# A cross-attention kernel's fill: one set of context values beside each of the first three slots, and the output weights loaded two slots later

## The chip, the cores and the metric

The kernel runs on one core of one Trainium2 chip. The metric is the device time of the whole kernel in microseconds (us), lower is better; a time of a kernel is the median of several runs. Before the change it is 1691.91 us, the median of three runs from 1691.86 to 1692.5 us.

## The reference

For 32 batches, hidden states of 512 rows by 640 columns attend to a context of 77 rows by 1024 columns, with 20 heads of 32 columns. Everything is float32.

```python
end = N_TXT                                   # 77
ehs_txt = encoder_hidden_states[:, :end]      # all the rows that there are
q = _heads(hidden_states @ to_q_w)
h_txt = _sdpa(q, _heads(ehs_txt @ to_k_w), _heads(ehs_txt @ to_v_w))
...
out = _merge(h_txt) + SCALE_OBJ * _merge(h_obj) + SCALE_OTH * _merge(h_oth) + SCALE_IP * _merge(h_ip)
out = out @ to_out_w + to_out_b
out = (out + residual) / RESCALE
```

The context has 77 rows, so the slices for the other three attentions are empty and add zeros. What is left is: queries, keys and values from three projections, softmax over 77 keys for each of 20 heads, the weighted values, an output projection, a bias and the residual.

## The kernel before, in words

**Precision.** Every large product is made from operands split into a high part (rounded to the matmul format) and a low part (the remainder); a product is three matmuls, high by high, high by low and low by high. ScalarE (ACT) makes the high part, VectorE (DVE) or GpSimd (POOL) the low one.

**Context first.** The 2464 context rows are taken in five groups (four of 512, the last of 416). For each group the keys (tile pk) and the values (tile pv) of five chunks of 128 columns, that is four heads each, are made on TensorE (PE) and put into DRAM (`k_dram`, `v_dram`). One chunk's values of a group are `context_values(g, j, psv)`: 24 matmuls, then a transposition on DVE into tile vs (`split_values`) and four DMAs from POOL's queue to `v_dram`. The value weights lie in two tiles, wv_s0 for chunks 0 to 2 and wv_s1 for chunks 3 and 4. Values of the last group are not needed before the last batches, and are put between the first steps of the attention.

**Attention by units.** A unit n is four heads of one batch: n = 5 b + j for batch b and chunk j, 160 units. The steps of a unit:
- `queries(n)`: 15 matmuls into tile pq, copied to tile qt (`copy_q`).
- `scores(n)`: 16 small matmuls into four PSUM banks, one a head. The banks are usually the four of tag sc; table `LENT` names the units for which some heads lie in a bank of tag po or pa.
- `maxima(n)` on DVE (tile nm), then `exps(n, i)` for head i: four exponentials on ACT into tile pn; a bank is free once the exponentials of its head are done.
- `normalize(n)`: a reciprocal on DVE (rs) that needs all of the unit's exponentials, and a product on POOL.
- `transpose_p(n)`: DVE transposes pn into tile z. There are two of each, pn0, z0 for even n and pn1, z1 for odd n.
- `move_p(n)`: four DMAs from SP's queue carry z into tile raw (two buffers), and so over the partitions.
- `values(n)`: four matmuls of raw with the batch's values (vb) into a bank pa; `high_a` on ACT and `low_a` on DVE split it into tile at, after which the bank is free.
- the output projection of a batch (`group`), from at and the output weights wo_s, which come from `wo_dram` by five DMAs (`load_wo`).

**Order.** The order is written by hand: an engine carries out its instructions in the order in which the code names them. Units 0 to 7 are the fill: `slot(n)` makes the scores of unit n, the queries of n + 1 and, from n = 3 on (`LAG`), the values of n - 3. From unit 8 (`FIRST`) on, `window(n)` takes two units at a time, 76 times, and `end()` closes. In the slots 3 to 6 (`copied`) `transpose_p(n - 1)` and `move_p(n - 1)` stand behind the copy of the queries. Memory is handed on by pools: wo_s lies where wv_s0 was, z1 and raw lie where wv_s1 and the context tiles ct were, and each waits for the last reader of what it lies on. In the kernel before, the last group's values are placed so: chunks 0 and 1 ahead of slot 0, chunk 2 in slot 0, chunks 4 and 3 in slot 1, none in slot 2. `load_wo` is called in slot 1, and slot 3's scores use one bank po, one pa and two sc.

Of the kernel before, what the change touches and what calls it, by code (L numbers as in the profile page):

```python
# [37 lines left out]
def kernel(  # L38
# [30 lines left out]
    NC_ = C // P  # L69
# [136 lines left out]
    def values_of(g, j, pool):  # L206

        for k in range(NK):
            values_of_chunk(g, j, k, pool)

    def split_values(g, j, between=None):

        g0, gn = GROUPS_KV[g]
        na = gn // Q
        vs = kvp.tile([P, G // Q, HD], F32, tag="vs", name="vs", bufs=3)
        nc.vector.transpose(vs[:, :na], pvs.pop(j)[:, :gn].rearrange("p (a d) -> p a d", d=HD))
        if between is not None:
            between()
        dst = v_dram[g0 : g0 + gn, j].rearrange("(a t) i d -> i t a d", t=Q)
        engine = nc.gpsimd if g == LAST else nc.sync  # L220
        for i in range(HPC):
            engine.dma_start(dst[i], vs[i * Q : (i + 1) * Q, :na])

    def context_values(g, j, pool):
        values_of(g, j, pool)
        split_values(g, j)
# [10 lines left out]
    def load_x(b, quarters=range(4)):  # L237

        if b not in xss:
            xss[b] = natural()  # L240
        xs = xss[b]
        src = x[b].rearrange("(a j) (q u) -> q j a u", j=Q, q=4)
        for q in quarters:
            nc.sync.dma_start(xs[q * Q : (q + 1) * Q, :, :], src[q])
# [64 lines left out]
    LAST, split_ks = len(GROUPS_KV) - 1, []  # L309
# [79 lines left out]
    psv = tc.alloc_tile_pool(name="psv", bufs=3, space=PSUM, side="right", reuse_waits="tile")  # L389
# [28 lines left out]
    def load_keys(b):  # L418
        nc.sync.dma_start(kbs[b % 2], k_dram[:, :, b * NKEY : (b + 1) * NKEY])

    def load_values(b):
        rows = v_dram[b * NKEY : b * NKEY + KPAD]
        nc.sync.dma_start(
            vbs[b % 2].rearrange("p j h d -> p (j h d)"),
            rows.rearrange("(c i) j h d -> i c (j h d)", i=Q),
        )

    def bank(tag):
        pool, bufs = (ps, {"sc": 4, "pq": 1}[tag]) if tag in ("sc", "pq") else (late[1], {"po": 1, "pa": 2}[tag])
        return pool.tile([P, S], F32, tag=tag, name=tag, bufs=bufs)  # L430
# [17 lines left out]
    def copy_q(n, copy=nc.scalar.copy):  # L448
        copy(qt_of(n), pqs.pop(n))  # L449
# [13 lines left out]
    def scores(n):  # L463
        banks = [bank(LENT.get(n, {}).get(i, "sc")) for i in range(HPC)]
        views = [sc.rearrange("p (t k) -> p t k", t=NQ)[:, :, :NKEY] for sc in banks]
        for t in range(NQ):
            for i in range(HPC):
                scs[n, i, t] = views[i][:, t]
                score(views[i][:, t], n, i, t)
        return views  # L470

    def maxima(n, views):
        for i in range(HPC):
            nm = nmt[:, (n % 2 * HPC + i) * NQ : (n % 2 * HPC + i + 1) * NQ]
            nc.vector.tensor_reduce(nm, views[i], AX.X, ALU.max, negate=True)
            for t in range(NQ):
                nms[n, i, t] = nm[:, t : t + 1]
# [53 lines left out]
    def transpose_p(n):  # L531

        pn, z = pnb[n % 2], zs[n % 2]
        nc.vector.transpose(  # L534
            z.rearrange("p c h t j -> p (h t) c j"),
            pn.rearrange("p a (c i) -> p a c i", i=Q),
        )

    def move_p(n):

        raws[n] = late[0].tile([KPAD, NQ, HPC, P], F32, tag="raw", name="raw", bufs=2)
        for a in range(4):
            nc.sync.dma_start(
                raws[n][:, a].rearrange("p h q -> p (h q)"),
                zs[n % 2][a * Q : (a + 1) * Q].rearrange("i c h t j -> i c (h t j)"),
            )
# [23 lines left out]
    def low_a(n):  # L570
        at = ats[n]
        nc.vector.tensor_tensor(
            at[:, 1, :], pas.pop(n), at[:, 0, :].bitcast(F32), ALU.subtract
        )
# [75 lines left out]
        elif h == 1:  # L650
            nc.sync.dma_start(out[last, rows, :], xr)

    LATE, LAG = 2, 3
    EARLY_X = {4: 0, 6: 1}
    LENT = {3: {0: "po", 1: "pa"}, 4: {2: "po", 3: "pa"}, 6: {2: "po", 3: "pa"}}
    held, wos = [], []

    def take(m, tag="pa"):
# [4 lines left out]
    def load_wo(ks):  # L663
        for k in ks:
            nc.sync.dma_start(wos[0][:, k].bitcast(F32), wo_dram[:, k].bitcast(F32))

    def slot(n, beside=()):
        b, j = divmod(n, NC_)
        copied, last = 3 <= n <= 6, n == FIRST - 1
        views = scores(n)  # L670
        maxima(n, views)
        while held:
            low_a(held.pop())
        if n and not copied and not last:
            transpose_p(n - 1)
        if n == 1:
            load_wo(range(3))
        if j == 0:
            load_keys(b + 1)
        if j == 1:  # L680
            load_values(b)
        if n == 1:
            load_wo(range(3, NC_))
        if n == 0:
            load_x(2)
            load_y(0, range(4))
        for i in range(2):
            exps(n, i)
        if last:
            transpose_p(n - 1)  # L690
        if n >= LATE and not last and not copied:
            move_p(n - 1)
        if len(beside) > 1:
            context_values(LAST, beside[1], psv)
        queries(n + 1, "po" if last else "pq")
        copy_q(n + 1, nc.vector.tensor_copy)
        if copied:
            transpose_p(n - 1)
            move_p(n - 1)
        if n >= LAG and not last:  # L700
            values(n - LAG)
        if last:
            qts.append(late[0].tile([P, S], F32, name="qt1"))
            queries(n + 2)
            copy_q(n + 2, nc.vector.tensor_copy)
        for i in range(2, HPC):
            exps(n, i)
        if not last:
            normalize(n)
        if n == 1:  # L710
            for i in range(NQ):
                transpose_x(2, i)
        if beside:
            context_values(LAST, beside[0], psv)
        if n >= LAG and not last:
            high_a(n - LAG)
            held.append(n - LAG)
        if n in EARLY_X:
            split_x(2, EARLY_X[n])
        if n == 3:  # L720
            load_bias()
        if n < 3:
            split_x(1, n + 2)
# [156 lines left out]
    for c in range(2):  # L880
        split_x(1, c)
    context_values(LAST, 1, psv)
    slot(0, (2,))
    kva.release()
    lw = ctx.enter_context(tc.tile_pool(name="lw", bufs=1, reuse_waits="tile"))
    wos.append(lw.tile([P, NC_, 2, C], FPR, name="wo_s"))
    slot(1, (3, 4))
    psv.release()
    kvp.release()
    late.append(ctx.enter_context(tc.tile_pool(name="late", bufs=1, reuse_waits="tile")))  # L890
# [2 lines left out]
    )  # L893
    zs.append(late[0].tile(ZSHAPE, F32, name="z1"))
    move_p(0)
    for n in range(LATE, FIRST):
        slot(n)
    for n in range(FIRST, N, 2):
# [42 lines left out]
```

## Time and profile before

| | |
|---|---|
| median of three runs | 1691.91 us |
| the profiled execution's own time | 1692.86 us |
| span of its profile | 1690.8 us |
| context stage (keys and values of the first four groups, keys of the last) | 0 to 249.7 us |
| first queries and the values of chunks 0 and 1 | 249.7 to 262.3 us |
| fill, slots 0 to 7 | 262.3 to 323.4 us |
| a window (two units) in the steady part | 17.63 us (scores at 323.37 and at 341.00) |
| busy share of the span: PE, DVE, ACT, POOL | 100%, 60%, 64%, 59% |

The span runs from the first to the last instruction of one profiled execution; 2.06 us of that execution lie outside it. Rows of the timeline give the start and the duration of one instruction or of a run of equal ones, both in us; in square brackets stands how long the engine was idle before it and what ended the wait. Ends of matmuls are modelled, so intervals between starts are the safer reading.

### The profile page before, as it was taken

How to read it: one execution, taken by the hardware profiler on the slowest of the kernel's cores; microseconds unless marked ns; L12 is line 12 of the kernel's file. 1: busy time of each engine (PE TensorE's matmuls, PEld its weight loads, DVE VectorE, ACT ScalarE, POOL GpSimd, SP SyncE). 2: the span in 40 equal slices, each digit the busy share in tenths (PEclk: the TensorE clock that was granted, in tenths of full speed). 3: DMA queues.
4: the chain of work that ended last, by engine and by line, in shares of the span. 5: the costliest groups of instructions: out<-in, count | busy, mean ns of one | idle time of the engine just before them, and what ended most of it. 6: DMA issues, size and time to landing. Idle time of an engine off the chain costs nothing.

```text
span 1690.8 us, 36827 instructions
## 1 busy us (share of the span) xinstructions
PE 1683.6 (100%) x12460; PEld 1303.9 (77%) x12460; DVE 1010.5 (60%) x1635; ACT 1075.9 (64%) x5622; POOL 990.1 (59%) x663
## 2 busy tenths in 40 slices
PE   9999999999999999999999999999999999999999
PEld 7888898777777777777777777777777777777777
DVE  4341235766676666766666657576666766667653
ACT  3231125867677676776767767677676776767762
POOL 1000026667667666667575766767667676766755
PEclk9999999999999999999999999999999999999999
DMA  9847558678889787879797988888979788888956
GB/s 182 159 94 189 121 103 229 150 173 188 190 187 204 172 204 175 202 181 212 166 211 166 211 181 195 185 194 186 203 173 204 173 202 190 188 192 183 210 136 187
DMA packets 363852, 306.51 MB, mean 181 GB/s; under 512 B 88784, under 2 KB 292112, under 8 KB 363664
## 3 DMA queue, kind: packets, MB, share of 16 engines
q1 hardware_dynamic: 360864, 296.61, 78.4%
q0 software_dynamic: 2704, 7.38, 1.4%
q8 instruction: 99, 1.62, 0.4%
q14 instruction: 89, 0.73, 0.1%
q10 hardware_dynamic: 96, 0.16, 0.0%
HBM read 120.36 MB, written 57.88 MB: 105 GB/s over the span
## 4 chain that ended last, share of the span: by engine, by line
PE 97%; DMA 1%; ACT 0%; DVE 0%; SPq 0%; issue 0%; POOL 0%; DVEq 0%; ACTq 0%
PE pq L437 32%; PE po L602 31%; PE pv L182 7%; PE pk L182 7%; PE sc L454 6%; PE po L553 4%; PE pq L553 4%; PE pa L454 3%; DMA wraw<-in_L_xattn_to_k_w_dram 1%; PE sc L634 1%; PE pa L553 0%; ACT pn L515 0%; DMA cs<-in_ctx_dram 0%; PE pa L634 0%; PE pq L602 0%; SPq L99 0%
## 5 line engine op out<-in xcount | busy, mean ns | idle before, releaser
L515 ACT ACTIVATE pn<-sc,nm 128x77 f32<-128x77 f32 x1928 | 597.3, 367 | 131.4 <-DVE nm L508 102.8
L437 PE MATMUL pq<-xt,wq_s 128*128 128x512 f32 x2349 | 559.0, 390 | 0.0
L602 PE MATMUL po<-at,wo_s 128*128 128x512 f32 x2295 | 554.6, 393 | 0.0
L437 PEld LDWEIGHTS pq<-xt,wq_s 128*128 128x128 f32 x2349 | 440.6, 188 | 91.4
L602 PEld LDWEIGHTS po<-at,wo_s 128*128 128x128 f32 x2295 | 425.1, 188 | 90.8
L515 ACT ACTIVATION_READ_ACCUMULATOR pn<-sc,nm 128x1 f32 x1928 | 477.3, 249 | 0.0
L527 POOL TENSOR_TENSOR pn<-pn,rs 128x1232 f32<-128x1232 f32 x160 | 363.6, 2273 | 125.3 <-DVE rs L525 121.8
L616 POOL TENSOR_TENSOR xs<-xs,ot 128x512 f32<-128x512 f32 x155 | 199.8, 1289 | 322.1 <-DVE ot L612 314.4
L534 DVE STREAM_TRANSPOSE z<-pn 128x1536 f32<-128x1536 f32 x160 | 282.3, 1765 | 113.7 <-POOL pn L527 92.2
L259 POOL TENSOR_TENSOR xt<-xs,xt 128x512 fp32r<-128x512 f32 x157 | 198.5, 1293 | 35.8 <-ACT xt L258 35.8
L515 ACT ACTIVATE pn<-pa,nm 128x77 f32<-128x77 f32 x620 | 200.5, 382 | 0.0
L587 POOL TENSOR_TENSOR xs<-xs,bias_y 128x640 f32<-128x640 f32 x124 | 192.4, 1574 | 0.2
L567 ACT CAST at<-po 128x512 fp32r<-128x512 f32 x77 | 45.1, 585 | 230.1 <-PE po L553 230.1
L508 DVE TENSOR_REDUCE nm<-sc 128x6 f32<-128x462 f32 x304 | 177.1, 624 | 15.2 <-PE pa L454 15.2
L449 DVE COPY qt<-pq 128x512 f32<-128x512 f32 x83 | 57.4, 691 | 210.1 <-PE pq L437 210.1
L454 PE MATMUL sc<-kb,qt 32*128 32x77 f32 x3856 | 161.9, 273 | 0.0
L515 ACT ACTIVATION_READ_ACCUMULATOR pn<-pa,nm 128x1 f32 x620 | 161.0, 263 | 0.0
L454 PEld LDWEIGHTS sc<-kb,qt 32*128 32x128 f32 x3856 | 149.4, 187 | 4.2 <-issue 2.2
L182 PE MATMUL pk<-ct,wk_s 128*128 128x512 f32 (+1 forms) x600 | 134.0, 382 | 0.7 <-ACT wk_s L89 0.5
L182 PE MATMUL pv<-ct,wv_s 128*128 128x512 f32 (+1 forms) x600 | 134.2, 382 | 0.0
L454 PEld LDWEIGHTS pa<-kb,qt 32*128 32x128 f32 x1240 | 83.9, 186 | 63.7 <-ACT at L567 63.7
L182 PEld LDWEIGHTS pk<-ct,wk_s 128*128 128x128 f32 x600 | 112.1, 188 | 20.9 <-ACT wk_s L89 1.2
(81 smaller groups left out, 1339.7 us busy)
## 6 DMA issues: line engine op xcount, KB each, us to landing
raw<-z SPq DMA_DIRECT2D x640, 192.0 KB, 3.4
xs<-in_x_dram SPq DMA_DIRECT2D x256, 320.0 KB, 6.3
out_dram<-xs SPq DMA_DIRECT2D x127, 320.0 KB, 4.8
vb<-v_dram SPq DMA_DIRECT2D x32, 240.0 KB, 4.4
kb<-k_dram SPq DMA_DIRECT2D x32, 192.5 KB, 4.6
cs<-in_ctx_dram SPq DMA_DIRECT2D x12, 512.0 KB, 9.0
k_dram<-ks POOLq DMA_DIRECT2D x20, 256.0 KB, 2.5
v_dram<-vs SPq DMA_DIRECT2D x80, 64.0 KB, 2.4
```

The source lines that it names most:

```text
L182: nc.tensor.matmul(held[j][:, :gn], w[:, k, a, :], cts[g, k][:, c, :gn], start=(k == 0 and n == 0), stop=(k == NK - 1 and n == 2),)
L259: low.tensor_tensor(parts[1], src, parts[0].bitcast(F32), ALU.subtract)
L437: nc.tensor.matmul(pqs[n], wq_s[:, k, a, j * P : (j + 1) * P], xts[b, k][:, c, :], start=(k == 0 and m == 0), stop=(k == NC_ - 1 and m == 2),)
L454: nc.tensor.matmul(out, qt_of(n)[r, t * P : (t + 1) * P], kbs[b % 2][r, j, :], start=True, stop=True, tile_position=(i * HD, 0),)
L508: nc.vector.tensor_reduce(nm, view, AX.X, ALU.max, negate=True)
L515: nc.scalar.activation(pnb[n % 2][:, at, :NKEY], scs.pop((n, i, t)), AF.Exp, bias=nms.pop((n, i, t)), accum_out=sms[n][:, at : at + 1],)
L527: nc.gpsimd.tensor_tensor(pf, pf, rs.unsqueeze(2).to_broadcast([P, NQ * HPC, NKEY]), ALU.mult)
L534: nc.vector.transpose(z.rearrange("p c h t j -> p (h t) c j"), pn.rearrange("p a (c i) -> p a c i", i=Q),)
L553: nc.tensor.matmul(pas[n][i * HD : (i + 1) * HD, :].rearrange("p (a q) -> p a q", q=P), vb[:, i, :], raw[:, :, i, :], start=True, stop=Tru ...
L587: nc.gpsimd.tensor_tensor(part, part, biases[1].unsqueeze(1).to_broadcast([P, 4, U]), ALU.add)
L602: nc.tensor.matmul(pos[b, c], wos[0][:, k, a, c * P : (c + 1) * P], ats[b * NC_ + k][:, d, :], start=(k == 0 and m == 0), stop=(k == NC_ - ...
L616: nc.gpsimd.tensor_tensor(part, part, ots.pop((b, c)).rearrange("p (a i) -> p a i", i=Q), ALU.add)
```

## The change

The last group's values of chunks 3, 4 and 2 stand in slots 0, 1 and 2, one set in each, at the place behind `normalize`. The output weights are loaded in slot 3 (three of five parts) and in slot 4 (two), behind `move_p`, where before all five were loaded in slot 1. Slot 3's scores use the four banks of tag sc. Since wv_s1 and ct are now read until slot 2 ends, z1 and raw exist only from there on: `transpose_p(1)` and `move_p(1)` stand between slot 2 and slot 3, where before they were in slot 2.

```diff
-    LATE, LAG = 2, 3
+    LATE, LAG = 3, 3
+    WO = {3: range(3), 4: range(3, NC_)}
     EARLY_X = {4: 0, 6: 1}
-    LENT = {3: {0: "po", 1: "pa"}, 4: {2: "po", 3: "pa"}, 6: {2: "po", 3: "pa"}}
+    LENT = {4: {2: "po", 3: "pa"}, 6: {2: "po", 3: "pa"}}
...
         while held:
             low_a(held.pop())
-        if n and not copied and not last:
-            transpose_p(n - 1)
         if n == 1:
-            load_wo(range(3))
+            transpose_p(0)
         if j == 0:
             load_keys(b + 1)
         if j == 1:
             load_values(b)
-        if n == 1:
-            load_wo(range(3, NC_))
...
-        if n >= LATE and not last and not copied:
-            move_p(n - 1)
-        if len(beside) > 1:
-            context_values(LAST, beside[1], psv)
         queries(n + 1, "po" if last else "pq")
         copy_q(n + 1, nc.vector.tensor_copy)
         if copied:
             transpose_p(n - 1)
             move_p(n - 1)
+        if n in WO:
+            load_wo(WO[n])
         if n >= LAG and not last:
             values(n - LAG)
...
-        if beside:
-            context_values(LAST, beside[0], psv)
+        for c in beside:
+            context_values(LAST, c, psv)
...
     context_values(LAST, 1, psv)
-    slot(0, (2,))
+    for n, c in enumerate((3, 4, 2)):
+        slot(n, (c,))
     kva.release()
     lw = ctx.enter_context(tc.tile_pool(name="lw", bufs=1, reuse_waits="tile"))
     wos.append(lw.tile([P, NC_, 2, C], FPR, name="wo_s"))
-    slot(1, (3, 4))
     psv.release()
     kvp.release()
...
     zs.append(late[0].tile(ZSHAPE, F32, name="z1"))
     move_p(0)
+    transpose_p(1)
+    move_p(1)
     for n in range(LATE, FIRST):
         slot(n)
```

How the instructions move, at three places. The number behind a tile's name tells two buffers apart: wv_s_82 is wv_s0, wv_s_83 is wv_s1; z_1877 and pn_1871 are z0 and pn0, z_2224 (now z_2283) and pn_1873 are z1 and pn1; qt_1875 is the one query tile of the fill.

PE from the scores of slot 0 to the first scores of slot 3, before:

```order
L454 MATMUL sc<-kb_1867,qt_1875 128x77 x16
L437 MATMUL pq<-xt,wq_s 128x512 x15
L182 MATMUL pv<-ct,wv_s_82 128x416 x24
L454 MATMUL sc<-kb_1867,qt_1875 128x77 x16
L182 MATMUL pv<-ct,wv_s_83 128x416 x24
L437 MATMUL pq<-xt,wq_s 128x512 x15
L182 MATMUL pv<-ct,wv_s_83 128x416 x24
L454 MATMUL sc<-kb_1867,qt_1875 128x77 x16
L437 MATMUL pq<-xt,wq_s 128x512 x15
L454 MATMUL po<-kb_1867,qt_1875 128x77
L454 MATMUL pa<-kb_1867,qt_1875 128x77
L454 MATMUL sc<-kb_1867,qt_1875 128x77 x2
```

and after the change, to the first values:

```order
L454 MATMUL sc<-kb_1867,qt_1875 128x77 x16
L437 MATMUL pq<-xt,wq_s 128x512 x15
L182 MATMUL pv<-ct,wv_s_83 128x416 x24
L454 MATMUL sc<-kb_1867,qt_1875 128x77 x16
L437 MATMUL pq<-xt,wq_s 128x512 x15
L182 MATMUL pv<-ct,wv_s_83 128x416 x24
L454 MATMUL sc<-kb_1867,qt_1875 128x77 x16
L437 MATMUL pq<-xt,wq_s 128x512 x15
L182 MATMUL pv<-ct,wv_s_82 128x416 x24
L454 MATMUL sc<-kb_1867,qt_1875 128x77 x16
L437 MATMUL pq<-xt,wq_s 128x512 x15
L553 MATMUL pa<-raw,vb_1869 32x512 x4
```

A set of values (pv) now stands between the queries and the scores three times; before, the last queries and the scores of slot 3 had nothing between them.

DVE from the scores' maxima of slot 2 to those of slot 3, before:

```order
L216 STREAM_TRANSPOSE vs<-pv 128x416
L475 TENSOR_REDUCE nm<-sc 128x4 x4
L534 STREAM_TRANSPOSE z_2224<-pn_1873 128x16x3x32
L449 COPY qt_1875<-pq 128x512
L525 RECIPROCAL rs<-sm 128x16
L475 TENSOR_REDUCE nm<-po 128x4
L475 TENSOR_REDUCE nm<-pa 128x4
L475 TENSOR_REDUCE nm<-sc 128x4 x2
```

and after:

```order
L216 STREAM_TRANSPOSE vs<-pv 128x416
L475 TENSOR_REDUCE nm<-sc 128x4 x4
L449 COPY qt_1875<-pq 128x512
L525 RECIPROCAL rs<-sm 128x16
L216 STREAM_TRANSPOSE vs<-pv 128x416
L534 STREAM_TRANSPOSE z_2283<-pn_1873 128x16x3x32
L475 TENSOR_REDUCE nm<-sc 128x4 x4
```

The last transposition of values and the one of unit 1's probabilities now stand directly ahead of the maxima of slot 3.

SP's queue of DMAs from the values of batch 0 on, before:

```order
L665 DMA wo_s<-wo_dram 128x1280 x3
L423 DMA vb_1869<-v_dram 96x1x640
L665 DMA wo_s<-wo_dram 128x1280 x2
L543 DMA raw<-z_1877 96x1x512 x4
L543 DMA raw<-z_2224 96x1x512 x4
L543 DMA raw<-z_1877 96x1x512 x4
L543 DMA raw<-z_2224 96x1x512 x4
L419 DMA kb_1867<-k_dram 128x5x77
```

and after:

```order
L423 DMA vb_1869<-v_dram 96x1x640
L543 DMA raw<-z_1877 96x1x512 x4
L543 DMA raw<-z_2283 96x1x512 x4
L543 DMA raw<-z_1877 96x1x512 x4
L666 DMA wo_s<-wo_dram 128x1280 x3
L543 DMA raw<-z_2283 96x1x512 x4
L666 DMA wo_s<-wo_dram 128x1280 x2
L419 DMA kb_1867<-k_dram 128x5x77
```

Three parts of the output weights now stand ahead of the move of unit 3, and two behind it.

## The prediction

> **What bounds the kernel now.** I read the page first, then who waited for whom from 240 to 330 us (PE appears there once), then the timeline of the fill engine by engine. The page's first part, and one row of the windows view for the steady part (its first two numbers are the length and PE's busy time), say who sets the end:
>
> ```profile
> PE 1683.6 (100%) x12460; PEld 1303.9 (77%) x12460; DVE 1010.5 (60%) x1635; ACT 1075.9 (64%) x5622; POOL 990.1 (59%) x663
> 323.30:1645.00 1321.70, 1321.70 (x10504) 1004.02 (x10500) 859.83 (x1391) 952.84 (x5173) 900.58 (x570) 1.00 0.83 188
> ```
>
> PE never stops in the windows, at a granted clock of 1.00. A change to the fill can therefore only shift the start of the windows; what reaches the first scores of window 8, at 323.37 us, reaches the end. Here is PE in the fill (start, duration, and in brackets a wait and what ended it):
>
> ```profile
> 262.28 1.13 PE L454 MATMUL sc<-kb,qt 32*128 32x77 f32 x32
> 263.34 3.68 PE L437 MATMUL pq<-xt,wq_s 128*128 128x512 f32 x15
> 266.86 4.69 PE L182 MATMUL pv<-ct,wv_s 128*128 128x416 f32 x24
> 271.48 1.13 PE L454 MATMUL sc<-kb,qt 32*128 32x77 f32 x32
> 272.54 4.75 PE L182 MATMUL pv<-ct,wv_s 128*128 128x416 f32 x24
> 277.13 3.58 PE L437 MATMUL pq<-xt,wq_s 128*128 128x512 f32 x15
> 280.55 4.69 PE L182 MATMUL pv<-ct,wv_s 128*128 128x416 f32 x24
> 285.17 1.13 PE L454 MATMUL sc<-kb,qt 32*128 32x77 f32 x32
> 286.23 3.68 PE L437 MATMUL pq<-xt,wq_s 128*128 128x512 f32 x15
> 290.69 0.33 PE L454 MATMUL po<-kb,qt 32*128 32x77 f32 x1 [0.78 <-DVE qt L449]
> 291.75 3.72 PE L437 MATMUL pq<-xt,wq_s 128*128 128x512 f32 x15
> ```
>
> From 262.28 us on the only idle time is 0.78 us before the scores of slot 3, whose query tile has to be copied by DVE. So the most that this stage can give is under a microsecond, 0.05% of the span. The differences that decide are differences of tenths, and the question is whether another engine lets PE keep them.
>
> **The change part by part.** *PE: the wait goes.* The same matmuls run, only their order differs, so I sum intervals between starts. Scores take 1.06 us (271.48 to 272.54), queries behind scores 3.52 (263.34 to 266.86), a set of values behind queries 4.62 (280.55 to 285.17). From slot 1's scores at 271.48 the new order is scores, queries, values, scores, queries, values: 2 x (1.06 + 3.52 + 4.62) = 18.40 us, so slot 3's scores start at 289.88. Before they start at 290.69: **-0.81 us**. Each copy of queries now hides under 4.62 us of values; without that cover it costs the 0.78 us again, per slot. The four sc banks that slot 3 now takes are read by unit 2's exponentials. Before, these end 6.73 us behind the start of their scores:
>
> ```profile
> 291.61 0.29 ACT L515 ACTIVATION_READ_ACCUMULATOR pn<-sc,nm 128x1 f32 x1
> ```
>
> (291.61 + 0.29 - 285.17). Slot 2's scores now start at 271.48 + 9.20 = 280.68, so the banks are free at about 287.4, 2.5 us ahead of use: the plain banks cost nothing.
>
> *DVE and ACT: no gain at slot 3.* Here is what they do around it:
>
> ```profile
> 271.58 0.62 DVE L216 STREAM_TRANSPOSE vs<-pv 128x416 f32<-128x416 f32 x1 [2.29 <-PE pv L182]
> 289.94 0.69 DVE L449 COPY qt<-pq 128x512 f32<-128x512 f32 x1 [0.31 <-PE pq L437]
> 292.10 0.42 DVE L475 TENSOR_REDUCE nm<-po 128x4 f32<-128x308 f32 x1
> 296.11 1.77 DVE L534 STREAM_TRANSPOSE z<-pn 128x1536 f32<-128x1536 f32 x1
> 297.81 0.21 DVE L525 RECIPROCAL rs<-sm 128x16 f32<-128x16 f32 x1
> 301.79 1.77 DVE L534 STREAM_TRANSPOSE z<-pn 128x1536 f32<-128x1536 f32 x1
> 311.06 0.68 DVE L572 TENSOR_TENSOR at<-pa,at 128x512 fp32r<-128x512 f32 x1
> ...
> 292.62 0.33 ACT L515 ACTIVATE pn<-po,nm 128x77 f32<-128x77 f32 x1 [0.20 <-DVE nm L475]
> 294.94 0.24 ACT L515 ACTIVATION_READ_ACCUMULATOR pn<-pa,nm 128x1 f32 x1
> 297.33 0.30 ACT L515 ACTIVATION_READ_ACCUMULATOR pn<-sc,nm 128x1 f32 x1
> 298.44 0.33 ACT L515 ACTIVATE pn<-sc,nm 128x77 f32<-128x77 f32 x1 [0.34 <-DVE nm L475]
> 306.56 0.36 ACT L515 ACTIVATION_READ_ACCUMULATOR pn<-sc,nm 128x1 f32 x1
> 313.61 0.26 ACT L515 ACTIVATION_READ_ACCUMULATOR pn<-po,nm 128x1 f32 x1
> ```
>
> The transposition of the last values starts 0.10 us behind the next start on PE (271.58 against 271.48), so at 289.98, and takes 0.54 in a queue (0.62 less an overlap of 0.08 that such rows show); unit 1's z then takes 1.70 (296.11 to 297.81). Both stand ahead of slot 3's maxima, which start at 292.22; the first exponential follows 0.52 later (292.10 to 292.62), at 292.74. That is 0.12 *later* than before, though PE is 0.81 earlier. From there ACT's chain feeds itself: exponentials, reciprocal, maxima, exponentials. Its last exponential of unit 3 ends at 297.33 + 0.30 + 0.12 = 297.75; before, the reciprocal at 297.81 waited for DVE's z, which is now early, so it follows at about 297.8 again, and the exponentials of unit 4 start at 298.4 as they did. ACT and what hangs on it then stand where they stood, and PE runs into them from an earlier place. PE's starts in the later slots:
>
> ```profile
> 295.40 1.07 PE L553 MATMUL pa<-raw,vb 96*32 96x512 f32 x8
> 301.08 1.07 PE L553 MATMUL pa<-raw,vb 96*32 96x512 f32 x8
> 307.75 0.34 PE L454 MATMUL sc<-kb,qt 32*128 32x77 f32 x2
> 312.44 1.07 PE L553 MATMUL pa<-raw,vb 96*32 96x512 f32 x8
> 314.49 1.66 PE L437 MATMUL po<-xt,wq_s 128*128 128x512 f32 x6
> 321.52 1.07 PE L553 MATMUL po<-raw,vb 96*32 96x512 f32 x8
> ```
>
> A release reaches PE 0.06 us behind the end of the work (copy 289.94 + 0.69 = 290.63, scores 290.69). Four places, in order:
> - Slot 4's scores, due at 296.39 - 0.81 = 295.58, need unit 3's second head: 294.94 + 0.24 + 0.12 + 0.06 = 295.36. No stop, 0.2 us to spare.
> - Slot 6's scores, due at 307.75 - 0.81 = 306.94, need unit 5's second head: 306.56 + 0.36 + 0.06 = 306.98. About 0.03 is given back.
> - The values of unit 3, due at 312.44 - 0.78 = 311.66, need the bank that DVE frees at 311.06 + 0.68 + 0.06 = 311.80. 0.14 is given back.
> - The queries into po, due at 314.49 - 0.64 = 313.85, need unit 6's third head: 313.61 + 0.26 + 0.06 = 313.93. 0.08 is given back.
>
> (296.39 is where the values at 295.40 end, one interval of 0.99.) Behind that, values, copies and at's split are waited for from PE's side, so the rest moves with PE. Sum: -0.81 + 0.03 + 0.14 + 0.08 = **-0.56 us**. Bounds: -0.81 if ACT's chain turns out a little earlier than I have it, 0 if it is later by as much again.
>
> *DMA: the moved weights.* These rows carry it: issue and landing of the weights' five DMAs, the same for raw, and the windows row of the weights' transfer (the last number is GB/s) and of a raw transfer alone:
>
> ```profile
> L665 SPq DMA_DIRECT2D wo_s<-wo_dram x5: 344/454/627, 271.6 to 274.4; - x5
> DMA to landing us min/median/max: 3.9/6.9/9.2
> ...
> raw<-z SPq DMA_DIRECT2D x640, 192.0 KB, 3.4
> ...
> L543 SPq DMA_DIRECT2D raw<-z x30: 571/600/2196, 285.3 to 329.5; - x30
> ...
> 274.00:282.00 8.00, 8.00 (x41) 7.38 (x40) 3.81 (x6) 4.72 (x29) 5.21 (x8) 1.00 1.02 392
> 306.00:308.00 2.00, 2.00 (x20) 0.77 (x22) 1.14 (x2) 2.00 (x16) 1.41 (x2) 1.00 1.00 246
> ```
>
> Raw 0 can go once chunk 4 has been read, at about 280.7, and is wanted at 294.6: hidden. Raw 1 goes when its z is done, 292.3, takes four issues of 0.6 and lands 3.4 later, at 298.1; it is wanted at 301.08 - 0.81 = 300.3. Raw 2, whose z ends at 296.11 + 1.77 - 0.81 = 297.07, is issued from 297.1 to 299.5 and is through by about 302. Then come three weights parts, issued by 301: 3 x 640 KB at 392 GB/s are 5.0 us, so until 307.1. Raw 3, whose z ends at 301.79 + 1.77 - 0.81 = 302.75, is issued by 305.2 and is behind them: 4 x 192 KB at 246 GB/s are 3.2 us, done at 310.3. It is wanted at 311.66. I cost the move at **nothing**, covered by 1.4 us; past that each microsecond costs one. The other two weights parts (3.3 us) then stand ahead of raw 4, done at 310.3 + 3.3 + 3.2 = 316.8, wanted at 321.52 - 0.56 = 321.0. If raw 3 shared the DMA engines with these two parts, it would be done at 307.1 + 3.2 + 3.3 = 313.6, and PE would be 1.2 us later than before instead of earlier (313.6 against 312.44). No row shows raw beside weights; I take the order of issue, since the four raw DMAs are issued ahead of the two.
>
> [...]
>
> **The rivals.** *First, ACT keeps all of the gain from PE.* If the maxima of slot 3 come 0.6 us later than worked out (the transposition of values waiting for its POOL transfers, say), slot 4's scores stop, and each later place moves by as much: -0.56 + 0.6, PE ends where it was. For it: ACT waits only 0.34 us ahead of unit 4's exponentials, so what is late there stays late. Against it: the transposition writes one of three buffers, and waits for the transfer of the set before last but one only. Time: 1691.9.
>
> *Second, slower: the weights get in raw 3's way.* Point: raw 3 landing later than 311.66. Sharing gave +1.2 us above. With the longest landing seen for the third weights DMA, 301 + 9.2 = 310.2, and the 3.2 us for raw 3 behind it, its values start at 313.4 instead of 312.44: +1.0 us, 1692.9. If the last two parts overtake it with that landing, 306.1 + 9.2 + 3.2 = 318.5, that is +6.1 us and 1698.0. For it: raw and the weights are on one queue and the rates are tight. Against: a 1.4 us cover, and the order of issue.
>
> *Third, the change does not do what it says*: slot 3's scores wait for something else, such as banks. Against it: the exponentials of unit 2 end 2.5 us before, as worked out. Time as in the first rival.
>
> **How the numbers follow.** The profiled span would become 1690.8 - 0.56 = 1690.24. The profiled execution, 1692.86 with 2.06 outside its span, lies 0.95 above the median of the runs, 1691.91; the shift is the same for both, so I forecast 1691.91 - 0.56 = 1691.35, rounded to **1691.3 us**, with 1691.0 to 1691.6 as this case's own range. Chances: the forecast 0.62; gain given back, with the third rival, 0.20; weights in the way by up to 3 us 0.13; by more 0.03; a gain of over 3.4 us 0.02, for which I see no mechanism. About what a measurement of this kernel can tell from no change is 0.2%, 3.4 us. So faster 0.02, within 0.2% 0.95, slower 0.03. The range runs from the full -0.81 with some spread of the runs, 1690.8, to the second rival's first price, 1692.9.
>
> **What would show it.** In the changed profile: no wait of PE for qt before slot 3's scores, these at 289.9; the first exponential of unit 3 at 292.7; short waits of PE at the values of unit 3; the first scores of window 8 at 322.8, and 17.63 us per window from there. The forecast is wrong if PE waits for raw anywhere in slots 3 to 7, if the exponentials of unit 3 start well off 292.7, or if a window's length changes.

## The result, and the profile after

| | before | change |
|---|---|---|
| median of eight runs each | 1692.10 us | 1697.65 us |
| lowest to highest | 1691.83 to 1692.59 | 1696.17 to 1699.98 |
| span of the profiled execution | 1690.8 | 1694.4 |
| slot 0's scores to the first scores of window 8 | 61.09 | 65.06 |

The change is slower: ratio 1.0036, 95% interval 1.0026 to 1.0045. The forecast was 1691.3 us, with a range from 1690.8 to 1692.9. The profiled execution of the change took 1696.41 us, near the low end of its runs; what the longer ones add comes with the fifth question below. PE stands still for raw in slot 6, which the forecast had named as a sign that it is wrong.

PE in the fill of the change (timeline: start, duration, and in brackets a wait and what ended it):

```profile
261.67 1.13 PE L454 MATMUL sc<-kb,qt 32*128 32x77 f32 x32
...
284.65 4.69 PE L182 MATMUL pv<-ct,wv_s 128*128 128x416 f32 x24
289.27 1.13 PE L454 MATMUL sc<-kb,qt 32*128 32x77 f32 x32
290.33 3.68 PE L437 MATMUL pq<-xt,wq_s 128*128 128x512 f32 x15
...
307.43 1.66 PE L437 MATMUL pq<-xt,wq_s 128*128 128x512 f32 x6
...
313.81 1.06 PE L553 MATMUL pa<-raw,vb 96*32 96x512 f32 x8 [2.66 <-DMA raw<-z]
...
324.88 1.06 PE L553 MATMUL po<-raw,vb 96*32 96x512 f32 x8 [1.91 <-DVE qt L449]
325.76 1.04 PE L553 MATMUL pq<-raw,vb 96*32 96x512 f32 x8
326.73 0.33 PE L454 MATMUL pa<-kb,qt 32*128 32x77 f32 x1
```

Slot 0 starts 0.61 us earlier than in the profile of before (261.67 against 262.28). That is the context stage, which the change does not touch, so all places are compared from slot 0's scores on. Slot 3's scores stand 27.60 us behind them, before 28.41: 0.81 sooner, as forecast. The gain is there up to slot 6. Then PE stops twice, 2.66 us for raw of unit 3 and 1.91 us at unit 4, and 2.66 + 1.91 less the gain of 0.6 is the 3.97 us by which window 8 is later (65.06 less 61.09). Behind that nothing differs: PE's busy time over the 76 windows is 1321.66 us, before 1321.70.

The first stop names raw. The second names DVE's copy of the queries, and DVE's timeline says what the copy stood behind:

```profile
313.80 1.78 DVE L534 STREAM_TRANSPOSE z<-pn 128x1536 f32<-128x1536 f32 x1 [1.92 <-DMA raw<-z]
...
322.47 1.78 DVE L534 STREAM_TRANSPOSE z<-pn 128x1536 f32<-128x1536 f32 x1 [4.28 <-DMA raw<-z]
324.17 0.65 DVE L449 COPY qt<-po 128x512 f32<-128x512 f32 x1
```

DVE may not write z0 for unit 6 before the move of unit 4 has read it, and the copy is queued behind that transposition. Both stops are late moves, as the chain of waits from 296 to 330 us shows (start and duration, here from issue to landing):

```profile
303.50 9.39 DMA raw<-z
312.89 0.02 issue
312.91 9.44 DMA raw<-z
```

These are one DMA of unit 3's move and one of unit 4's; the second is issued when the first has landed. The trace shows why: SP's DMAs take eight semaphores in turn, and here each issue waits until the DMA issued eight places before it has landed. Unit 4's z was written by 307.78 (306.01 + 1.77), but its first DMA waited for the semaphore of the third weights part, which landed at 310.46, and was issued at 310.54; the other three, issued at 311.18, 312.09 and 312.91, each waited for one of unit 3's, landed at 311.15, 312.08 and 312.89. SP's queue (start and duration of the issues), and from the view of the tile raw the four issues of unit 3's move with their landing:

```profile
291.71 7.32 SPq L543 DMA_DIRECT2D raw<-z  x8
299.35 1.91 SPq L666 DMA_DIRECT2D wo_s<-wo_dram  x3
302.17 2.81 SPq L543 DMA_DIRECT2D raw<-z  x4
305.02 1.84 SPq L666 DMA_DIRECT2D wo_s<-wo_dram  x2
307.95 0.57 SPq L419 DMA_DIRECT2D kb<-k_dram  x1
310.54 2.94 SPq L543 DMA_DIRECT2D raw<-z  x4
```

```profile
L543 SPq DMA_DIRECT2D raw<-z x4: 577/689/722, 302.2 to 304.3; - x4
DMA to landing us min/median/max: 9.0/9.3/9.4
```

In the fill of before such a DMA of unit 3 landed 3.2 us after its issue (median of four); here it takes 9.3. The issue itself is on time: unit 3's z is done at 302.1, and the first DMA goes out at 302.17. The windows view of the same 20 us shows why there is no room (the last two numbers are the busy share of the DMA engines and GB/s), before and after:

```profile
298.00:318.00 20.00, 20.00 (x179) 14.08 (x178) 16.32 (x31) 19.43 (x116) 12.53 (x10) 1.00 0.69 164
```

```profile
298.00:318.00 20.00, 17.34 (x167) 11.86 (x166) 15.56 (x28) 18.85 (x111) 11.77 (x9) 1.00 1.02 281
```

The DMA engines went from 0.69 busy to full (1.02).

### The profile page after: what moved, and what is told of

It reads as the page before. It is cut to its first block, busy times and chain, and to the rows that moved or that the text cites. A ratio compares the mean times of both kernels' runs of the same rounds, so it can differ in the third digit from the quotient of the medians.

```text
span 1694.4 us, 36822 instructions
## 1 busy us (share of the span) xinstructions
PE 1682.7 (99%) x12460; PEld 1303.4 (77%) x12460; DVE 1010.9 (60%) x1635; ACT 1078.1 (64%) x5622; POOL 991.2 (58%) x663
## 4 chain that ended last, share of the span: by engine, by line
PE 96%; DMA 2%; SPq 1%; DVE 0%; ACT 0%; issue 0%; POOL 0%; DVEq 0%; ACTq 0%
PE pq L437 31%; PE po L602 31%; PE pv L182 7%; PE pk L182 7%; PE sc L454 6%; PE po L553 4%; PE pq L553 4%; PE pa L454 3%; DMA raw<-z 1%; DMA wraw<-in_L_xattn_to_k_w_dram 1%; PE sc L634 1%; SPq L99 0%; ACT pn L515 0%; DMA cs<-in_ctx_dram 0%; PE pa L634 0%
```

## The experiments

Twelve runs were made, one of them of the change itself once more. One table first, since the same quantities decide most of them. "Ahead" is the number of parts of the weights (640 KB each) that stand in SP's queue between the moves of units 2 and 3; "landing" is the median of unit 3's four DMAs from issue to landing; the next two columns are counted from slot 0's scores, in us. All columns but the last are of one profiled execution. The runs come from several chips; the kernel before took 1692.10 to 1692.53 us on them.

| kernel | ahead | landing | values of unit 3 | window 8 | PE's stops | median or single time (runs) |
|---|---|---|---|---|---|---|
| before | 0 | 3.2 | 50.16 | 61.09 | 0.78 | 1692.10 (8) |
| change | 3 | 9.3 | 52.14 | 65.06 | 2.66, 1.91 | 1697.65 (8) |
| g3, all in slot 7 | 0 | 3.2 | 49.55 | 60.51 | (wo_s) | 1698.58 (1) |
| g2, two and three | 0 | 3.0 | 49.55 | 60.52 | none | 1692.26 (11) |
| e3, one a slot | 1 | 4.2 | 49.57 | 60.55 | none | 1691.85 (11) |
| h1, two ahead | 2 | 7.7 | 50.53 | 61.47 | 1.08 | 1693.20 (1) |
| e2, weights alone, in before | 3 | 8.6 | 52.17 | 66.29 | 0.79, 1.99 | 1696.13 (7) |
| e4, last two later | 3 | 9.5 | 52.44 | 66.25 | 2.98 | 1697.35 (6) |
| f3, nothing behind | 3 | 9.4 | 52.25 | 66.35 | 2.80 | 1697.42 (1) |
| g1, bias later | 3 | 8.1 | 50.96 | 63.53 | 1.51 | 1696.04 (1) |
| f4, change again | 3 | 9.8 | 52.60 | 66.70 | 3.15 | 1698.11 (1) |
| f2, one behind each of units 0 to 4 | 1 | 8.3 | 51.03 | 64.93 | 1.05, 0.51, 0.47, 2.20 | 1698.91 (9) |

**First question: is it the weights or the new order of PE and DVE?** Three kernels. The first puts the weights back:

```diff
-    WO = {3: range(3), 4: range(3, NC_)}
+    WO = {}
...
-    for n, c in enumerate((3, 4, 2)):
-        slot(n, (c,))
+    slot(0, (2,))
     kva.release()
...
+    slot(1, (3,))
+    slot(2, (4,))
```

(and `load_wo` in slot 1 as before).

> The change with its chunks as 2, 3, 4 in slots 0, 1, 2 (so that the memory of the output weights is free after slot 0) and the weights loaded in slot 1 as before; the order on PE, the plain banks and z1 stay as in the change. Measure: from the start of slot 0's scores to the first scores of window 8 (before 61.09 us, change 65.06 us). Theory (the moved weights slow the moves of units 3 and 4): 60.3 to 60.6 us, no wait of PE for raw, time 0.5 us below the kernel before. Rival (the new order of PE, DVE and banks costs the time, the waits for raw only happen to end last): 64 to 65 us, time 4 to 6 us above.

Measured: 1697.87 us (six runs, ratio 1.0032, interval 1.0021 to 1.0044), 66.40 us to window 8. My expectation missed, and neither theory is what happened. PE and SP's queue:

```profile
297.03 1.94 PE L553 MATMUL pa<-raw,vb 96*32 96x512 f32 x8 [2.93 <-DMA raw<-z]
```

```profile
271.06 1.30 SPq L666 DMA_DIRECT2D wo_s<-wo_dram  x3
272.41 0.64 SPq L423 DMA_DIRECT2D vb<-v_dram  x1
273.09 1.19 SPq L666 DMA_DIRECT2D wo_s<-wo_dram  x2
289.46 10.77 SPq L543 DMA_DIRECT2D raw<-z  x10
```

The stop is at the values of unit 0. With chunk 4 in slot 2, the memory under raw is read until 289.4 us, and unit 0's move is issued at 289.46 instead of 280.17. The chunk order 3, 4, 2 frees raw's memory early and that of the weights late; 2, 3, 4 the other way round. This run is no test of the weights, but it shows why the change needs its order, and the weights with it their late place.

The second moves the weights alone, in the kernel before:

```diff
+    WO = {3: range(3), 4: range(3, NC_)}
...
-        if n == 1:
-            load_wo(range(3))
...
-        if n == 1:
-            load_wo(range(3, NC_))
...
             move_p(n - 1)
+        if n in WO:
+            load_wo(WO[n])
```

> The kernel before, with nothing changed but the place of the output weights: three parts in slot 3, two in slot 4, behind the moves. Theory (moved weights): unit 2's and unit 3's moves stand 0.8 us later behind slot 0 than in the change, so raw of unit 3 lands 52.0 us behind slot 0's scores and is wanted at 50.16: PE waits 1.9 us there and again for unit 4; the first scores of window 8 come 65 to 66 us behind slot 0's scores, time 4 to 6 us above the kernel before. Rival (order of PE, DVE and banks): 61.1 us, time unchanged.

Measured: 1696.13 us (seven runs, ratio 1.0022, interval 1.0012 to 1.0033), window 8 at 66.29, PE's stop 1.99 us at unit 3. The weights' move alone makes a loss of this kind, 3.75 us in the medians where the change loses 5.55; the expected second stop was not there, for a reason that the fifth question gives.

The third leaves the new order and takes the weights out of every move's way:

```diff
-    WO = {3: range(3), 4: range(3, NC_)}
+    WO = {7: range(NC_)}
```

> The change with all five parts of the weights in slot 7, behind unit 5's move, so that no move of the fill has any of them ahead. Theory T: no wait of PE for raw, 60.5 us from slot 0's scores to the first scores of window 8 (-0.56 as forecast for PE and ACT); the weights then land late for the first output projection, and PE waits 0 to 6 us for wo_s there. Rival (the moves are slow in the new order even without weights ahead): waits for raw in slots 4 to 7, over 62 us to window 8.

Measured: 60.51 us to window 8, 0.58 less than before, with no wait for raw; unit 3's DMAs land in 3.2 us again. The order of PE and DVE gives what was forecast. The time is lost later, at the first output projection:

```profile
327.67 0.97 PE L602 MATMUL po<-at,wo_s 128*128 128x512 f32 x3 [1.91 <-DMA wo_s<-wo_dram]
...
331.37 1.62 PE L602 MATMUL po<-at,wo_s 128*128 128x512 f32 x3 [2.73 <-DMA wo_s<-wo_dram]
```

**Second question: does the delay go with the bytes ahead?** One part a slot, and two parts ahead:

```diff
-    WO = {3: range(3), 4: range(3, NC_)}
+    WO = {n: (n - 3,) for n in range(3, 8)}
```

> The change with one part of the output weights in each of the slots 3 to 7 instead of three and two. Theory (bytes of weights in flight beside a move delay it): one part is 640 KB, 2.3 us at 280 GB/s; raw of unit 3, 312.9 in the change, comes 3 to 4.5 us sooner and is in time; no wait of PE for raw, 60.3 to 61.0 us from slot 0's scores to window 8, time 0 to 0.6 us below the kernel before. Rival (each weights DMA on SP's queue costs the next move its place or its semaphore, whatever its bytes): waits at several units, 62 to 64 us.

Measured: the profiled execution has no wait and 60.55 us to window 8, as expected. But of 11 runs six lie between 1691.36 and 1691.85, one each at 1692.78 and 1693.96, and three between 1697.40 and 1700.66 with a mean clock of 0.998 or 0.997. Median 1691.85 against 1692.38, ratio 1.0009, interval 0.9996 to 1.0022: undecided. Unit 5's move landed 5.0 us after its issues and 0.6 us before PE wanted it. That this margin fails in the three long runs is a guess; none of them was profiled.

```diff
+    WO = {3: (0, 1), 7: (2, 3, 4)}
```

> The change with two parts of the weights in slot 3 ahead of unit 3's move (three in the change), none in slot 4, three in slot 7. Each part takes 1.7 us at 392 GB/s (the forecast's rate) or 2.5 us at 262 (the rate seen in the change), so raw of unit 3 lands 1.7 to 2.5 us sooner than the 51.2 to 52.2 us behind slot 0's scores of the change: 48.7 to 50.5, wanted at 49.5; PE waits 0 to 1.1 us, no half clock, 60.5 to 61.6 us to window 8. If the delay were not in proportion to the bytes ahead (a queue that blocks as soon as weights stand in it), it lands past 51 and PE waits 2 us or more.

Measured: 50.53 us for the values of unit 3, a stop of 1.08 us, window 8 at 61.47: at the late end of what was expected. With 0, 1, 2 and 3 parts ahead the landing is 3.2, 4.2, 7.7 and 9.3 to 9.8 us. The delay grows with the bytes ahead, but not in proportion: the steps are 1.0, 3.5 and some 2 us. A single part is nearly free, since in e3 it has landed at 43.30, soon after unit 3's last DMA is issued (42.41). In f2 below one part at this place is not free: it stands behind two earlier ones, lands at 47.41, and unit 3's DMAs land after 8.3 us.

**Third question: does what stands behind a move in the queue slow it?** The forecast chose between an order and a sharing of the DMA engines. First the last two parts go from slot 4 to slot 5:

```diff
+    WO = {3: range(3), 5: range(3, NC_)}
```

> The change with its first three parts of the weights in slot 3 as they are, the last two in slot 5 instead of slot 4, so that nothing stands behind unit 3's move. Theory S (DMAs of one queue that are in flight share the bandwidth): unit 3's raw lands 1.5 to 2.5 us sooner than the 51.2 us behind slot 0's scores of the change, PE's wait of 2.66 us there shrinks to 0.2 to 1.2; no wait for unit 4; 60.7 to 61.9 us to window 8. Theory T (only what is issued ahead delays a DMA): unit 3's raw lands where it did, PE waits 2.6 us as in the change; unit 4's wait goes; 62.8 to 63.3 us.

Measured: PE stops 2.98 us, unit 3's DMAs land in 9.5, the values start 52.44 behind slot 0's scores: no sooner than in the change. The median is 1697.35 us (six runs, ratio 1.0032, interval 1.0020 to 1.0044), and window 8 stands at 66.25, later than either theory had it; the half clock of the fifth question came with the stop. Since the keys of batch 2 now followed at once, the next kernel takes these away too:

```diff
+    WO = {3: range(3), 6: range(3, NC_)}
...
-        if j == 0:
-            load_keys(b + 1)
+        if n in (0, 6):
+            load_keys(1 + n // 5)
```

> The change with its first three parts of the weights in slot 3 as they are, the last two in slot 6, and the keys of batch 2 loaded in slot 6 instead of slot 5: nothing stands behind unit 3's move in the queue until unit 4's. Theory S (DMAs issued later share the bandwidth): unit 3's raw lands 49.4 to 50.2 us behind slot 0's scores (51.2 in the change), PE waits 0 to 0.7 us. Theory T (only what is issued ahead counts): it lands where it did, PE waits 2.5 us or more.

Measured: landing 9.4 us, a stop of 2.80. Nothing stood behind the move until unit 4's own, issued from 46.19 us on, and it is as late as ever. On the landing of unit 3's move theory T holds in both runs: the order of issue decides, as the forecast had assumed, not the sharing.

**Fourth question: do other transfers slow the weights?** The bias (four DMAs of 20 KB from POOL's queue) is moved away:

```diff
-        if n == 3:
+        if n == 7:
             load_bias()
```

> The change with the load of the bias (four small DMAs from POOL's queue, issued at 300 to 302 us beside the weights) moved from slot 3 to slot 7. Theory B (the three parts ahead of unit 3's move run at some 260 GB/s instead of 392 because the bias is in flight beside them): unit 3's raw lands 1.5 to 2.5 us sooner, 49.5 to 50.7 us behind slot 0's scores, PE waits 0 to 1.2 us. Theory T alone (what is ahead in SP's queue, at this rate anyway): it lands 51.2 to 52.2 us behind slot 0's scores, PE waits 2.6 to 3.2 us as in the two profiles of the change.

Measured: landing 8.1 instead of 9.3 and 9.8, the values of unit 3 1.2 and 1.6 us sooner than in the two profiles of the change, a stop of 1.51. Part of the delay is thus the bias, somewhat less than expected, as far as one run without it can tell (with it, the change, f3, f4 and e4 lie between 52.14 and 52.60). From 300 to 308 us the DMA engines moved 295 GB/s with the bias and 296 without it, so the mean rate is not what it slows. The trace shows what is later: it has 16 updates of a semaphore for each DMA (20224 for the 1264 DMAs on SP's eight semaphores in the change), and the last of them is what counts here as the landing. For the third weights part they come from 46.28 to 48.79 us behind slot 0's scores in the change, and from 46.02 to 47.73 without the bias. So the first update moves by 0.3 us and the last by 1.1. Why a few are late is not shown.

**Fifth question: why do many runs take 1 to 4 us more than the profiled one?** The change was profiled once more:

> The change itself, unedited, for another profiled execution. Theory: if its time is over 1697 us, the page shows a clock below 1.000, half a clock for 6.8 us behind one of the two stops of PE, and the time above 1696.2 us is 3.4 us for each such stretch. If it is near 1696.2 us, the clock is 1.00. Rival: the longer time is spread over the windows or lies in the context stage.

Measured: 1698.11 us. PE's stop at unit 3 is 3.15 us, and the windows view shows the granted clock (the number ahead of the last two):

```profile
314.06 1.06 PE L553 MATMUL pa<-raw,vb 96*32 96x512 f32 x8 [3.15 <-DMA raw<-z]
...
316.87 2.93 PE L437 MATMUL po<-xt,wq_s 128*128 128x512 f32 x6
```

```profile
312.00:314.00 2.00, 0.00 (x0) 0.00 (x0) 0.00 (x0) 2.00 (x15) 0.00 (x0) 1.00 0.99 320
314.00:316.00 2.00, 1.94 (x28) 1.13 (x32) 1.91 (x2) 1.11 (x4) 0.00 (x0) 0.81 1.07 344
316.00:318.00 2.00, 2.00 (x23) 1.67 (x20) 1.07 (x3) 0.78 (x4) 1.90 (x1) 0.50 1.09 241
318.00:320.00 2.00, 2.00 (x6) 1.54 (x5) 1.16 (x3) 2.00 (x15) 1.61 (x2) 0.50 1.10 255
320.00:322.00 2.00, 2.00 (x6) 1.59 (x5) 0.00 (x0) 2.00 (x15) 0.00 (x0) 0.50 0.92 244
322.00:324.00 2.00, 2.00 (x10) 1.61 (x10) 1.59 (x1) 0.53 (x4) 0.00 (x0) 0.98 0.55 155
```

The clock falls to half 1.2 us after PE has gone on, for 6.83 us by the trace's record of it; six queries take 2.93 us instead of 1.66. PE is then so slow that unit 4's move is in time, and the second stop is gone; that is also what happened in e2. Window 8 stands at 66.70, 5.61 us later than before, and the medians differ by 5.55. The time is 1.9 us above 1696.2 and not 3.4, as the second stop is gone. The execution profiled first, of 1696.41 us, has both stops and a clock of 1.000. Of the other seven runs six, from 1697.13 us on, have a mean clock of 0.998 or 0.997 (6.83 us at half clock make 0.998 in f4), and the shortest, 1696.17, has 0.999. Where in these runs the half clock lies was not profiled.

To see that the stop makes the half clock, and which stops do, the kernel before was given stops of growing length:

```diff
             queries(n + 3)
+            for _ in range(n // 2 % 10):
+                nc.vector.tensor_copy(qt_of(n + 3), pqs[n + 3])
             copy_q(n + 3, nc.vector.tensor_copy)
```

> The kernel before, with the copy of the queries at each window's end done again 0 to 9 times (the same values; window by window in turn), so that PE stops ahead of the next scores for about 0.61 us per copy less 1.0 us of cover: from 0 to 4.5 us, 76 windows. Theory (a stop that leaves PE idle for about 2 us or more of a fixed stretch of 3.4 us halves the granted clock for 6.8 us, 3.4 us of work): no halving at stops below 1.5 us, some at 2 to 3, all above 4; 25 to 38 halvings, the time 140 us of stops and 85 to 130 us of halvings above the kernel before. Rival (the half clock seen in three profiles has another cause than the stop): clock 1.00 everywhere, about 140 us above.

Measured: 2150.18 us, mean clock 0.889. The extra copies took more than expected, so the stops sum up to 235.7 us, not 140, and there were 54 halvings where 25 to 38 had been expected: every stop of about 2 us and more had one. Two of the stops, of 1.24 and 1.96 us, and the clock behind each:

```profile
536.17 1.06 PE L553 MATMUL pq<-raw,vb 96*32 96x512 f32 x8 [1.24 <-DVE qt L449]
...
555.98 1.07 PE L553 MATMUL pq<-raw,vb 96*32 96x512 f32 x8 [1.96 <-DVE qt L449]
```

```profile
535.00:539.00 4.00, 2.83 (x72) 1.99 (x72) 2.92 (x7) 1.17 (x2) 2.27 (x1) 1.00 0.78 177
539.00:543.00 4.00, 4.00 (x25) 3.27 (x22) 3.80 (x6) 3.05 (x21) 0.00 (x0) 1.00 0.16 40
```

```profile
554.00:557.00 3.00, 1.04 (x15) 0.18 (x12) 2.56 (x5) 0.59 (x1) 1.24 (x2) 1.00 0.60 121
557.00:560.00 3.00, 3.00 (x64) 3.00 (x60) 1.14 (x3) 2.14 (x4) 3.00 (x3) 0.52 0.95 253
560.00:563.00 3.00, 3.00 (x18) 2.38 (x15) 2.42 (x4) 1.68 (x11) 2.12 (x2) 0.50 0.93 244
563.00:566.00 3.00, 3.00 (x13) 2.41 (x12) 1.66 (x3) 3.00 (x22) 0.00 (x0) 0.84 0.61 147
```

Over the whole trace, the 14 stops of 0.51 and 1.24 us were followed by no half clock, and all 54 stops from 1.96 to 6.31 us by one, of 6.83 us (22 times) or 10.24 us (32 times). That is 478 us at half clock. In 31 us of it PE still stood, so the work lost is half of the other 447, 224 us, which with the 235.7 us of stops gives 459; the kernel became 458 us longer. In this run such a stop thus cost about twice its length on average. The stops of one length recur every 235.5 us, which is 69.0 times 3.41 us, half of the shorter stretch. Ends of half clocks keep to the same step; here are two more of them, in rows of the windows view:

```profile
403.20:403.60 0.40, 0.40 (x2) 0.30 (x2) 0.00 (x0) 0.40 (x4) 0.00 (x0) 0.57 0.00 0
```

```profile
483.00:486.00 3.00, 3.00 (x8) 2.38 (x9) 3.00 (x4) 2.32 (x15) 0.00 (x0) 0.59 0.00 0
```

With half clock up to the end and full clock behind it, a row's mean gives the end: 403.54 and 485.46 us here, 563.96 in the row from 563 to 566 above. They lie 24.0 and 23.0 times 3.41 us apart. So all repeats of a stop fall at one phase of that step, and the limit between 1.24 and 1.96 us holds for these phases; the stops of 2.66 and 1.91 us in the first profile of the change left the clock at 1.00.

**Sixth question: is there a place where the weights do no harm?** First one part behind each of the moves of units 0 to 4; a second kernel, further down, has two parts and three:

```diff
+    WO = {n: (n - 1,) for n in range(3, 6)}
...
     move_p(0)
+    load_wo((0,))
     transpose_p(1)
     move_p(1)
+    load_wo((1,))
```

> The change with one part of the output weights behind each of the moves of units 0 to 4, so that one goes in the idle of SP's queue between units 0 and 1, one between 1 and 2, and none behind unit 5. Theory (a move is late by what stands ahead of it in its queue; unit 5's had 0.6 us to spare with a part behind it): no wait of PE for raw, 60.5 us from slot 0's scores to window 8, and no execution with a lower clock: all runs within 1 us, median 0.4 to 0.8 us below the kernel before. Rival (long executions of the run with one part a slot come from elsewhere, such as the order of PE and DVE): some executions 5 to 9 us longer here too.

Measured: 1698.91 us (nine runs, 1692.65 to 1703.00, ratio 1.0038, interval 1.0026 to 1.0051): no better than the change's own placing (ratio 1.0036), and my expectation fell. Unit 2's DMAs landed 7.4 us after their issue, unit 3's 8.3, unit 4's 8.9. PE stopped briefly from unit 2 on and longest at unit 5:

```profile
325.56 1.06 PE L553 MATMUL pq<-raw,vb 96*32 96x512 f32 x8 [2.20 <-DMA raw<-z]
```

Each slot of 5.7 us carries a move; with weights in the queue from the start the DMA engines do not catch up (1.04 busy from 298 to 318 us), and the delay grows up to unit 4.

```diff
+    WO = {4: (0, 1), 7: (2, 3, 4)}
...
-        if j == 0:
-            load_keys(b + 1)
+        if n == 0:
+            load_keys(1)
...
             load_wo(WO[n])
+        if n == 7:
+            load_keys(2)
```

> The change with two parts of the weights in slot 4 behind unit 3's move (ahead of unit 4's, which has 4 us to spare), three in slot 7 behind unit 5's, and the keys of batch 2 behind these. Theory T: units 1 to 3 have nothing ahead, unit 4's raw lands at about 316, in time; no wait of PE for raw or wo_s, 60.5 us to window 8, all executions within 1.5 us of each other at a clock of 1.000, median 0.4 to 0.8 us below the kernel before. Rival (the DMA engines are full from unit 1's move on, so that a move is late in some executions wherever the weights stand): some executions 4 to 9 us longer, with a clock below 1.000.

Measured: no stop, 60.52 us to window 8, all 11 runs between 1690.93 and 1693.34 at a clock of 1.000. The two parts stand ahead of unit 4's move, which lands in 6.0 us, 4.1 us before PE wants it. Median 1692.26 us, and that of before on the same chip 1692.26 as well (15 runs, 1691.16 to 1692.84): ratio 1.0001, interval 0.9992 to 1.0010. The 0.57 us are in the profile and not in the medians, where 0.4 to 0.8 us had been expected; the runs spread over 2.4 us, and slot 0 alone starts at 261.67 in one profile here and at 262.28 in another. So the change can be had without its loss, but no version was shown to beat the kernel before.

## Why the prediction was wrong

**Right: PE and ACT.** The wait ahead of slot 3's scores is gone (-0.81, measured 28.41 less 27.60). The first exponential of unit 3 starts at 292.11, on before's clock 292.72, and 292.74 was forecast; the queries of slot 6 follow 0.77 us sooner than before (45.76 against 46.53 behind slot 0), where 0.81 less 0.03 was forecast, and where no move is late the values of unit 3 0.61 sooner (49.55 against 50.16), forecast 0.64. The sum of -0.56 is what three kernels show that keep the new order and have no move late: 60.51, 60.52 and 60.55 against 61.09. The first rival (ACT keeps the gain) and the third (the change does not do what it says) did not happen.

**Wrong: "3 x 640 KB at 392 GB/s are 5.0 us, so until 307.1".** On this term stood "done at 310.3" and "I cost the move at **nothing**, covered by 1.4 us". The three weights DMAs took 8.6 us. Here are the issue of the third in the change, and all five with their time to landing (it grows from each to the next, so the least is the first's and the median the third's):

```profile
300.83 0.43 SPq L666 DMA_DIRECT2D wo_s<-wo_dram  x1
...
L666 SPq DMA_DIRECT2D wo_s<-wo_dram x5: 430/587/1207, 299.3 to 305.7; - x5
DMA to landing us min/median/max: 5.7/9.6/13.0
```

By the trace the last DMA of raw 2 landed at 301.89, the three weights DMAs at 305.02, 307.93 and 310.46, and the four of raw 3 at 311.15, 312.08, 312.89 and 313.67. On before's clock, 0.61 us later, the forecast's own sum reads: raw 2 through at 302.5 (302.1 by the forecast), the weights 8.6 us (5.0), raw 3 behind them 3.2 us (3.2), together 314.3 (310.3). Raw was wanted at 311.66, so a cover of 1.4 us became a lack of 2.6, and PE's first stop is 2.66 us. The term for raw 3 was right; the term for the weights was not. All nine profiles with weights between these moves say the same: raw 3's last DMA lands 2.8 to 3.5 us behind the last of them. And the weights take, from raw 2's last landing, 3.0 us for one part (e3), 6.8 for two (h1) and 8.1 to 9.0 for three with the bias beside them, where the forecast had 1.7 for each.

Part of the 3.6 us that were missing can be named. The row with 392 GB/s is not of the weights alone, since POOL's transfers to `v_dram` and the load of vb run in it too. Read as landings, the quoted rows say (274.4 + 9.2) - (271.6 + 3.9) = 8.1 us for four parts, 2.0 us each: 6.1 us for three, and a cover of 0.3 us. The bias, which the forecast had not counted, makes about 1.0 us: without it, in g1, the three parts took 7.6 us. The remaining 1.5 us no run explains. What the trace does show is that the weights now end unevenly: the 16 updates of the third part lie within 0.44 us in before and are spread over 2.5 us in the change.

A fixed time for each DMA is not the missing term. The first DMA of unit 3 in before was issued at 303.62 and landed at 306.27, 2.65 us later; its packets ran from 304.85 to 305.98, so 1.23 us passed ahead of them and 0.3 us behind. In the full queue of the change raw 3's DMAs landed 0.7 to 0.9 us apart, right behind the weights, without such a time added.

**The sharing.** The forecast dismissed it, and rightly: in e4 and f3, with the two parts moved away from behind it, unit 3's move landed after 9.5 and 9.4 us, no sooner than with them in the change (9.3 and 9.8). That its figure, 313.6, lies near the 314.3 measured is chance. What did not follow from the order of issue is that raw would be in time.

**The second rival happened, at more than its price of +1.0 us.** Its first sum was close: 301 + 9.2 = 310.2 for the third weights DMA, where 300.83 + 9.63 = 310.46 was measured, and 3.2 us for raw 3 behind it. The values of unit 3 came 1.98 us later than before (52.14 against 50.16). Two consequences were in no part of the prediction. A late move delays the next: unit 4's was forecast for 316.8 and landed at 322.35 (312.91 + 9.44), 322.96 on before's clock, since its issues waited for the landing of the DMAs eight places before them (310.46 to 312.89) and two more weights parts stood ahead of it; through z0 and DVE's queue it made the second stop. And a stop of PE can have a half clock behind it (6.83 us in f4, 3.41 in g1), which in f1 cost about as much as the stops did (224 us and 235.7). Weights in the way had a chance of 0.16, and 0.03 of it for more than 3 us, which is what came: 3.97 us in the first profile and 5.55 in the medians. That was too little for a cover of 1.4 us on a queue that was to be full.

## What to carry to other kernels

A transfer behind others in SP's queue landed here after the last one ahead, by the time of its own bytes: 3.2 us for the four DMAs, as forecast, and 2.8 to 3.5 us in all nine profiles. What has to be estimated with care is the landing of those ahead. Take it from issues and landings of such transfers and not from the best rate in a row that others share: 392 GB/s made 5.0 us of what took 8.6. Before bulk is moved into a stage, compare the stage's DMA share with what is added: here 0.69 became 1.02, and in g2 bulk was harmless ahead of a move that had 4 us to spare. In this kernel, where PE is busy all the time, a stop of some 2 us could cost 3.4 us again in clock (6.83 us at half, behind 1.96 us in f1 and 3.15 us in f4), so covers of about a microsecond are not worth half a microsecond of gain.

## What the runs showed of the hardware

The clock fell to half after a stop of 1.51 us in g1 (for 3.41 us), and after all stops of 1.96 us and more in f1. The lengths of the half clock, 3.41, 6.83 and 10.24 us, are one, two and three times 3.41, and three ends of it in f1 lie 24.0 and 23.0 times 3.41 us apart. If a stop counts by how it lies to these steps, that would explain why 2.66 us passed in one profile of the change and 3.15 us did not in the other; this is an estimate of mine, as the phase itself was not varied by any run.

Issue to landing of unit 3's 192 KB DMAs went from 3.2 to 9.8 us with up to 1.9 MB ahead of them, and 80 KB of bias from another queue moved it by more than a microsecond, in one run without it, while the mean rate stayed at 295 GB/s. The 16 semaphore updates of the third weights part, the last of which is its landing, lay within 0.44 us in before and spread over 2.5 us in the change.
